# Gather buffers of a sparse graph layer, and the place where a sign matrix is made

## The chip, the cores and the metric

The kernel runs on one core of a Trainium2 chip. The metric is the device time of one execution in microseconds (us); less is better. A core has five engines that each run their own stream of instructions in order: TensorE (PE), VectorE (DVE), ScalarE (ACT), GpSimd (POOL) and SyncE (SP), which wait for each other through semaphores. SP, ACT and POOL also issue DMAs.

## The reference, cut to what matters

Four graph layers, each wrapped as `x = layernorm(x + layer(x, adj))`, on 2708 nodes with 512 features. `adj` is sparse: a random pattern with the diagonal set, weights from 0.05 to 1, float32.

```python
# layer 0
adj_hat = adj + eye;  d = 1 / sqrt(adj_hat.sum(axis=1))
return (d[:, None] * adj_hat * d[None, :] @ x) @ W.T + b
# layer 1
head = (adj > 0);  head = head / max(sqrt(sum(head * head, axis=-1)), 1e-12)
inc = adj + head
return (inc @ x) / sum(inc, axis=-1)
# layer 2 (attention over the neighbours, two gates)
h = x @ W_sa;  scores = (h @ a_sa[0, :512])[:, None] + (h @ a_sa[0, 512:])[None, :]
e = where(adj != 0, exp(-leaky_relu(scores, 0.01)), 0)
x_a = e / (sum(e, axis=1) + 1e-5) @ h;   x_b = adj @ (x @ W_gcnb) + b_gcnb
return sigmoid(attn_a * x_a + attn_b * x_b)   # attn_*: gates from adj @ x and x
# layer 3
bw = sign(weight);  ba = max(sign(x), 0)
return relu(adj @ (ba @ bw.T))
```

The sign matrix of this text is `bw`, 512 x 512, kept as bfloat16; `weight` comes transposed as `w3_t`.

## The kernel before, in words

The 2708 rows are cut into 22 blocks of 128 (the last one, number 21, has 20 rows). Layers handle them in the order `sequence = [0, 1, 21, 2, ..., 20]`. Nothing is multiplied as a dense 2708 x 2708 matrix: for each block of destination rows the kernel gathers only those source rows that the block's columns of `adj` use.

Stage 0 reads `adj`, counts and finds the non-zeros, writes the lists of source rows (`index`), gathers the used rows of the transposed `adj` into `packed` (one tile of 128 sources by 128 destinations for every gathered group), and projects `x` to `y_rows` in DRAM. The order inside this stage is written out (`in_order`); everywhere else each engine's order is made by a list scheduler from the order of the code, the dependencies and the buffers that pools have free. An operation that the code names late can therefore be put early if its buffers and inputs allow it.

Layer 0 and layer 1 have the same core. `gathered` (L626) takes a buffer of the pool's tag `xg` and issues an indirect DMA from POOL, which fetches 128 rows of 512 floats (256 KB) from `y_rows` (layer 0) or `x1_rows` (layer 1; the profile names all of the three `x*_rows` arrays `x_rows`). `add_tile` (L1393) multiplies the tile of `adj` with them into a PSUM tile of the block; a buffer is free again when this product is done. The number of `xg` buffers is the pool's `bufs`: 10 in `s_l0`, 8 in `s_l1`. After every third (layer 0) or second (layer 1) gather, POOL does a short memset (L636) as a pause. Blocks 0 and 1 of the sources are held in SBUF and need no gather.

Beside the products, layer 0's loop runs pieces of other work out of a dictionary `between`, keyed by the step: loads and columns for the attention of layer 2, the counts of positive elements that layer 1 needs (`count_positive`: DVE writes the 0/1 tile `pos` (L1185) and PE counts it, L1187), and `signs(k)` for k = 0 to 3 in steps 8, 10, 12 and 14. `signs` loads a quarter of `w3_t` (256 KB) on ACT's queue into a buffer of the tag `xb` (two of them, pool `work`), and DVE makes the signs in two operations, L1437 (is less than 0) and L1438 (is greater than 0, minus that). `grow1` (L1450 to L1454) adds, a block at a time, to layer 1's sums for block 0, whose sources are all nodes. t (L1508) is layer 0's sum plus the old features; its layer norm follows (L688 to L704).

Layer 1's loop: incidence tiles on DVE (L1674, L1675), products on PE, `finish1` (L1587, the layer norm, the write to `x2_rows`), and for the block before it `project1`: transposes (L1612), the product with `W_sa` (L1619), copies of `h` (L1625 on ACT, L1626 on DVE) and its write (L1627). `grow2` (L1652, L1653) adds to layer 2's sums for block 0.

Layer 2 gathers rows of `x2_rows` with 1028 floats (features, `h` and scores; 514 KB and more for a gather of 128) in `gathered_2` (L1820) into seven buffers and two spare places. `prepare` makes attention weights: ACT adds scores (L1575), DVE does the leaky step (L1576) and the mask (L1578, L1579), ACT the exp (L1580). `accumulate` multiplies both halves of each gathered row (L1844), `transpose2` (L1876) and `project2` (pc L1889, pg and pc L1892) use `W_gcnb` from `s_wg`, 1 MB loaded by ACT's queue at the layer's start (L1724); `finish2` uses the gates, and `sign_product` (L1953) multiplies the signs of the new features with `bw` and writes `xw_rows`. `open_block` makes the row `sl` of left scores (L1553, L1555), and `prepare_own` loads `h_own` on SP's queue. Layer 3 gathers rows of `xw_rows`.

Of the kernel before, what the change touches and what calls it, by code (L numbers as in the profile page):

```python
# [8 lines left out]
F32 = mybir.dt.float32  # L9
F32R = mybir.dt.float32r  # L10
BF16 = mybir.dt.bfloat16
# [3 lines left out]
ALU = mybir.AluOpType  # L15
# [4 lines left out]
P = 128  # L20
# [50 lines left out]
def dense_layers(  # L71
# [30 lines left out]
    NG = -(-N // W)  # L102
    CH = 3
    NFULL = N // P
# [12 lines left out]

    parts = [(j, min(CH, NFULL - j), P) for j in range(0, NFULL, CH)]
    if N % P:
# [53 lines left out]
    def load_until(k: int):  # L173
        while issued[0] <= min(k, 4 * PER_LAYER - 1):
# [3 lines left out]
            w = width(g)  # L178
            t = stream.tile([P, CH, W], F32, tag="adj", name=f"adj{i}")
            nc.sync.dma_start(  # L180
# [327 lines left out]
def sparse_layers(ctx, tc, x, adj, adj_t, w0_t, b0, w_sa, a_sa, w_gcnb, b_gcnb, wa, ba, wb, bb, w3_t,  # L508
# [11 lines left out]
    nc = tc.nc  # L520
    N, D = x.shape
    KC = D // P
    NB = -(-N // P)
# [19 lines left out]
    f = [feat.tile([P, D], F32, tag=f"f{b}", name=f"f{b}") for b in range(NB)]  # L543
# [175 lines left out]
    with tc.tile_pool(name="s_pre", bufs=1) as pre:  # L719
# [65 lines left out]
        turn_at, at = {}, 0  # L785
# [555 lines left out]
    work = ctx.enter_context(tc.tile_pool(name="s_work", bufs=2, side="right", reuse_waits="tile"))  # L1341

    w2 = ctx.enter_context(ExitStack())
    wp = w2.enter_context(tc.tile_pool(name="s_w2", bufs=1, side="right", reuse_waits="tile"))
    bw = wp.tile([P, KC, D], BF16, name="s_bw")
    sequence = [0, 1, NB - 1, *range(2, NB - 1)]


# [56 lines left out]
    with tc.tile_pool(name="s_l0", bufs=10, reuse_waits="tile") as lp:  # L1405
# [24 lines left out]
            for c, side in enumerate((1, 0)):  # L1430
                nc.vector.tensor_copy(wsa[:, :, D + c], vec[:, side, :])

        def signs(k: int):
            w3 = work.tile([P, D], F32, tag="xb", name=f"s_w3_{k}")
            nc.scalar.dma_start(w3, w3_t[k * P : (k + 1) * P, :])
            neg = lp.tile([P, D], F32, tag="scr", name=f"s_neg{k}", bufs=1)
            nc.vector.tensor_scalar(neg, w3, 0.0, None, op0=ALU.is_lt)  # L1437
            nc.vector.scalar_tensor_tensor(  # L1438
                bw[:, k, :], w3, 0.0, neg, op0=ALU.is_gt, op1=ALU.subtract
            )  # L1440

        nc.vector.memset(own1[:, 0:1], 1.0)
        grown1 = []

        def grow1(j: int):
# [14 lines left out]
        between = {  # L1460
            2: [attention_loads], 4: [lambda: attention_columns(0)],
            5: [lambda: attention_columns(1)], 6: [attention_sides],
            8: [lambda: signs(0)], 10: [lambda: signs(1)], 12: [lambda: signs(2)],
            14: [lambda: signs(3)],
        }
        def several(*actions):
            def act():
# [15 lines left out]
        for at, b in enumerate(sequence):  # L1483
# [23 lines left out]
            t = work.tile([P, D], F32, tag="t", name=f"t0_{b}")  # L1507
# [32 lines left out]


    state = {}

    def old_new(b: int):
        return tuple(pairs.get(b, (f[b], f[b])))
# [44 lines left out]
        layernorm(new[:m, :D], t, m, f"1_{b}", on_act=True)  # L1590
        nc.sync.dma_start(x2_rows[b * P : b * P + m, :D], new[:m])

    with tc.tile_pool(name="s_l1", bufs=8, reuse_waits="tile") as lp:
        def gate_columns(dst, c: int, pool, tag: str):

            pv = pool.tile([P, D], F32, tag=tag, name=f"pv2_{c}")
            nc.tensor.transpose(pv[:, : 2 * KC], vrows[:, c, :], ident[: 2 * KC, : 2 * KC])
            nc.vector.tensor_copy(
                dst.rearrange("p k t -> p t k"),
                pv[:, : 2 * KC].rearrange("p (t k) -> p t k", t=2),  # L1600
            )

        gate_columns(wsa[:, :, D + 2 :], 0, ps_mm, "mm")
        H = D // 2
        hs = {}

        def project1(j: int):

            m = rows(j)
            pt = ps_mm.tile([P, KC, P], F32, tag="sum0", name=f"xt1p_{j}", bufs=1)  # L1610
            for k in range(KC):
                nc.tensor.transpose(pt[:, k, :m], f[j][:m, k * P : (k + 1) * P], ident[:m, :m])  # L1612
            xt = lp.tile([P, KC, P], F32, tag="xt1", name=f"xt1_{j}", bufs=2)
            nc.scalar.copy(xt[:, :, :m], pt[:, :, :m])  # L1614
            p0 = ps_acc.tile([P, D], F32, tag="a1", name=f"h0_{j}")
            p1 = ps_acc.tile([P, D], F32, tag="e1", name=f"h1_{j}")
            for ps, w in ((p0[:m, :H], wsa[:, :, :H]), (p1[:m, : H + EXTRA], wsa[:, :, H:])):
                for k in range(KC):
                    nc.tensor.matmul(  # L1619
                        ps, xt[:, k, :m], w[:, k, :], start=(k == 0), stop=(k == KC - 1)  # L1620
                    )
            h = kept[j] if j < 2 else lp.tile(
                [P, D + EXTRA], F32, tag="h", name=f"h_{j}", bufs=4
            )
            nc.scalar.copy(h[:m, :H], p0[:m, :H])  # L1625
            nc.vector.tensor_copy(h[:m, H:], p1[:m, : H + EXTRA])  # L1626
            nc.sync.dma_start(x2_rows[j * P : j * P + m, D:], h[:m, : D + 2])  # L1627
            nc.vector.tensor_copy(cols[:m, j, :], h[:m, D:])
            hs[j] = h

        grown2 = []

        def grow2(js):

            r, n, st = rows(js[0]), len(js), state[0]
            e = lp.tile([P, G2, P], F32, tag="e0", name=f"e0_{js[0]}", bufs=2)[:r, :n, :]
            mask = lp.tile([P, G2, P], F32, tag="mask0", name=f"m0_{js[0]}", bufs=1)[:r, :n, :]
            a = packed[0][:r, js[0] : js[0] + n, :]
            weights_of(
                e, mask, [(e, mask, st["sl"][:r], a, [cols[:r, j, 0:1] for j in js])]  # L1640
            )
            for i in range(n):
                if grown2 or i:
                    nc.vector.tensor_tensor(
                        st["esum"][:r], st["esum"][:r], e[:, i, :], op=ALU.add
                    )
                else:
                    nc.vector.tensor_copy(st["esum"], e[:, i, :])
            for i, j in enumerate(js):
                at = dict(start=(not grown2), stop=(len(grown2) == NB - 1))  # L1650
                se, sa = st["sums"]
                nc.tensor.matmul(se, e[:, i, :], hs.pop(j)[:r, :D], **at)  # L1652
                nc.tensor.matmul(sa, a[:, i, :], f[j][:r], **at)  # L1653
                grown2.append(j)

        G2 = 2
        left = [(0, 1), (NB - 1,)] + [
            tuple(range(j, min(j + G2, NB - 1))) for j in range(2, NB - 1, G2)
        ]

        for at, b in enumerate(sequence):
            m = rows(b)
            if b:
                nd = len(direct(b))
                order_ = in_turns(b)
                src = {i: place_of_x(direct(b)[i]) for i in range(nd)}
                for i in order_:
                    if i >= nd:
                        src[i] = gathered(lp, D, x1_rows, b, i - nd)
                ps = ps_mm.tile([P, D], F32, tag="mm", name=f"l1_{b}")  # L1670
                inc_of = {}

                def incidence(iv, a, row):
                    nc.vector.scalar_tensor_tensor(iv, a, 0.0, row, op0=ALU.is_gt, op1=ALU.mult)  # L1674
                    nc.vector.tensor_tensor(iv, iv, a, op=ALU.add)  # L1675

                for i0, n in whole_runs(b, 3):
                    inc = lp.tile([P, 3, P], F32, tag="inc0", name=f"inc{b}_{i0}", bufs=3)
                    iv = inc[:, :n, :m]
                    incidence(  # L1680
                        iv, packed[b][:, i0 : i0 + n, :],
                        head_row[:, None, b * P : b * P + m].to_broadcast([P, n, m]),
                    )
                    for i in range(n):
                        inc_of[i0 + i] = iv[:, i, :]
                inc = lp.tile([P, P], F32, tag="inc1", name=f"incn{b}", bufs=3)
                for i0, r0, w, a in narrow_views(b):
                    n = a.shape[1]
                    at_ = b * P + r0
                    iv = inc[:, r0 : r0 + n * w].rearrange("p (n i) -> p n i", n=n)  # L1690
                    incidence(
                        iv, a,
                        head_row[:, at_ : at_ + n * w].rearrange("p (n i) -> p n i", n=n),
                    )
                    for i in range(n):
                        inc_of[i0 + i] = iv[:, i, :]
                for i in order_:
                    add_tile(ps, b, i, inc_of[i], src[i][:, :D], order_)
            else:
                ps = sum1  # L1700
            if left and left[0][-1] in sequence[: max(at - 2, 0)]:
                grow2(left.pop(0))
            finish1(b, ps)
            if at:
                project1(sequence[at - 1])
            if at == 1:
                open_block(0, wp2, ps_mm, "mm")
                open_sums(0)
        project1(sequence[-1])
        for js in left:  # L1710
            grow2(js)
# [5 lines left out]
    with tc.tile_pool(name="s_l2o", bufs=1, reuse_waits="tile") as op, \  # L1717
# [5 lines left out]
        wg = op.tile([P, KC, D + 2], F32, name="s_wg")  # L1723
        nc.scalar.dma_start(wg[:, :, :D], w_gcnb.rearrange("(k p) o -> p k o", p=P))  # L1724
        gate_columns(wg[:, :, D:], 1, ps_s2, "sm")
        CH = 3

        def parts_of_sums(b: int):
# [501 lines left out]
```

## Time and profile before

| | before |
|---|---|
| median of three runs | 988.28 us (986.34, 988.28, 994.11) |
| profiled execution | 992.0 us |
| span of its instructions | 990.3 us |
| mean granted TensorE clock | 0.946 |
| PE busy | 860.8 us, 87% of the span, 3659 instructions |
| DVE busy | 654.7 us, 66% |
| POOL busy | 549.4 us, 55% |
| ACT busy | 381.1 us, 38% |
| moved by DMA | 220.06 MB, mean 222 GB/s |
| the chain that ended last | PE 68%, DVE 14%, DMA 7%, issue 5%, ACT 2% |
| gathers of layer 0, of layer 1 | 98 of 997 ns, 98 of 978 ns on POOL |
| L1437 and L1438 | 4 each, 456 ns and 674 ns on DVE |

The stages in the trace: stage 0 to about 200 us, layer 0 to 352, layer 1 to 570, layer 2 to 870, layer 3 to the end.

How to read it: the profile is of one execution, so its durations are summed against 992.0 us, not against the median. "Busy" counts the time in which an engine runs an instruction. A wait has the form "waiting engine, what it was to make, its line <- releasing engine, what that made, its line"; a timeline line has its start, its duration, and in brackets the idle time of the engine before it with what ended that. "issue" is time in which an engine waited for nothing that the profile shows. Tile names are the program's with buffer numbers left out.

### The profile page before, as it was taken

The numbers are of one execution on the slowest core, as the hardware profiler recorded it, in microseconds if no ns is written. First come the engines' busy times: TensorE is split into PE (matmuls) and PEld (weight loads), VectorE is DVE, ScalarE is ACT, GpSimd is POOL, SyncE is SP. The second block draws the span as 40 slices with busy tenths as digits, with TensorE's granted clock in tenths as the row PEclk, the third lists the DMA queues.
The fourth block names the chain that finished last, engine by engine and source line by source line (L and its number), as shares of the span: only waits on it lengthen the run. The fifth ranks groups of instructions, "written<-read, shape, count | busy, mean of one in ns | idle before, by whom it ended". The sixth has DMA issues, their size and how long they took to land.

```text
span 990.3 us, 12880 instructions
## 1 busy us (share of the span) xinstructions
PE 860.8 (87%) x3659; PEld 452.2 (46%) x3659; DVE 654.7 (66%) x2538; ACT 381.1 (38%) x822; POOL 549.4 (55%) x660
## 2 busy tenths in 40 slices
PE   1898789759979979999999989988999999599992
PEld 0444344212222324555555634543555555378771
DVE  4888888726657766565654446675888776556685
ACT  2665556100000014554544433333444333254653
POOL 2577888687877647776542054553454320066661
PEclk9998998979989989999999998998999999889996
DMA  9999996466777646777653276786777541299985
GB/s 266 339 336 306 301 310 199 142 193 192 237 211 222 207 132 195 223 220 233 183 176 121 97 249 236 257 276 216 249 274 261 174 149 47 85 316 331 308 249 173
DMA packets 93557, 220.06 MB, mean 222 GB/s; under 512 B 13660, under 2 KB 28364, under 8 KB 93476
## 3 DMA queue, kind: packets, MB, share of 16 engines
q0 software_dynamic: 43008, 127.61, 43.5%
q1 hardware_dynamic: 38520, 76.78, 22.6%
q10 hardware_dynamic: 11948, 14.76, 4.7%
q8 instruction: 31, 0.51, 0.2%
q14 instruction: 50, 0.41, 0.1%
HBM read 178.21 MB, written 31.71 MB: 212 GB/s over the span
## 4 chain that ended last, share of the span: by engine, by line
PE 68%; DVE 14%; DMA 7%; issue 5%; ACT 2%; another core or an unknown queue 2%; POOL 1%; SPq 0%; ACTq 0%; DVEq 0%; POOLq 0%
PE l L1393 17%; PE h L1619 8%; PE e L1844 7%; PE a L1844 7%; PE l L2099 4%; PE pg L1892 4%; PE pc L1892 3%; PE y L1127 3%; PE l L2138 2%; PE l L1454 2%; PE e L1652 2%; PE a L1653 2%; PE px L1953 2%; DVE s_mask L895 2%; DMA xg<-x_rows,i 2%
## 5 line engine op out<-in xcount | busy, mean ns | idle before, releaser
L1093 POOL DMA_INDIRECT a<-in_adj_t_dram,row_at x98 | 111.3, 1136 | 58.7 <-DVE deg L838 26.1
L626 POOL DMA_INDIRECT xg<-x_rows,i x98 | 95.8, 978 | 70.7 <-PE l L1393 37.1
L626 POOL DMA_INDIRECT xg<-y_rows,i x98 | 97.7, 997 | 32.6 <-issue 19.0
L1393 PE MATMUL l<-xg,a 128*32 128x512 f32 (+3 forms) x196 | 86.0, 646 | 12.6 <-DMA xg<-y_rows,i 12.6
L1820 POOL DMA_INDIRECT xg<-x_rows,i x60 | 59.1, 986 | 61.8 <-ACT ae L1575 16.3
L1127 PE MATMUL y<-s_w,xt 128*128 128x512 f32 (+1 forms) x176 | 91.3, 667 | 1.7 <-ACT xt L1119 1.7
L626 POOL DMA_INDIRECT xg<-xw_rows,i x70 | 71.3, 1018 | 38.7 <-issue 15.9
L1820 POOL DMA_INDIRECT a<-x_rows,i x38 | 36.9, 970 | 95.1 <-DVE mask L1578 37.1
L1619 PE MATMUL h<-s_wsa,xt 128*128 128x256 f32 (+3 forms) x352 | 81.9, 385 | 0.0
L1619 PEld LDWEIGHTS h<-s_wsa,xt 128*128 128x128 f32 (+1 forms) x352 | 63.9, 186 | 24.8 <-ACT xt L1614 9.2
L830 ACT ACTIVATE unused<-arow 128x1408 uint8<-128x1408 f32 (+3 forms) x44 | 58.3, 1325 | 3.0 <-DMA x_rows<-s_zero 2.0
L663 ACT ACTIVATE rsqs<-mv 128x1 f32<-128x1 f32 (+2 forms) x56 | 11.3, 202 | 120.7 <-DVE mv L692 58.8
L1844 PE MATMUL a<-xg,a 128*32 128x512 f32 (+2 forms) x120 | 51.2, 629 | 4.3 <-DMA xg<-x_rows,i 4.3
L1127 PEld LDWEIGHTS y<-s_w,xt 128*128 128x128 f32 (+1 forms) x176 | 35.6, 213 | 41.9 <-issue 39.6
L2099 PE MATMUL l<-ws,pw 128*128 128x512 f32 (+1 forms) x210 | 50.8, 394 | 1.7 <-issue 1.2
L1844 PE MATMUL e<-xg,ae 128*32 128x512 f32 (+2 forms) x120 | 47.9, 601 | 1.1 <-issue 1.1
L694 POOL TENSOR_TENSOR rs<-mv,s_neg_half 128x1 f32<-128x1 f32 (+1 forms) x22 | 13.0, 592 | 61.4 <-DVE mv L692 52.0
L1892 PE MATMUL pg<-s_wg,pt 128*128 128x256 f32 (+1 forms) x176 | 45.0, 397 | 1.3 <-ACT pt L1880 1.3
L688 DVE BATCH_NORM_STATS2 st<-t 128x6 f32<-128x512 f32 (+1 forms) x66 | 45.3, 687 | 0.3
L916 PE MATMUL find<-s_sides,s_mask 128*128 128x5 bf16 (+1 forms) x462 | 15.7, 166 | 34.1 <-DVE s_mask L912 25.2
L2099 PEld LDWEIGHTS l<-ws,pw 128*128 128x128 f32 (+1 forms) x210 | 39.4, 190 | 11.9 <-issue 2.9
L1393 PEld LDWEIGHTS l<-xg,a 128*32 128x32 f32 (+3 forms) x196 | 19.8, 146 | 54.4 <-issue 38.6
(307 smaller groups left out, 1995.5 us busy)
## 6 DMA issues: line engine op xcount, KB each, us to landing
arow<-in_adj_dram SPq DMA_DIRECT2D x21, 704.0 KB
arow<-in_adj_dram SPq DMA_DIRECT2D x21, 650.0 KB
x_rows<-f SPq DMA_DIRECT2D x40, 256.0 KB
aw<-in_adj_t_dram SPq DMA_DIRECT2D x21, 320.0 KB
y_rows<-yt ACTq DMA_DIRECT2D x20, 256.0 KB
x_rows<-h SPq DMA_DIRECT2D x19, 257.0 KB
f<-in_x_dram SPq DMA_DIRECT2D x19, 256.0 KB
h_own<-x_rows SPq DMA_DIRECT2D x19, 256.0 KB
```

The lines of the kernel that those rows point to most:

```text
L626: nc.gpsimd.indirect_dma_start(out=t, out_offset=None, in_=src[:, :], in_offset=bass.IndirectOffsetOnAxis(ap=index[b][:, i : i + 1], axis=0),)
L688: nc.vector.bn_stats(st[:m], t[:m])
L830: nc.scalar.activation(unused[:m, : ar.shape[1]], ar, AF.Copy, accum_out=row_sums[:m, b, h : h + 1])
L895: nc.vector.tensor_scalar(mask[:m, c0 : c0 + ar.shape[1]], ar, 0.0, None, op0=ALU.not_equal)
L1093: nc.gpsimd.indirect_dma_start(out=packed[b][:, t + len(direct(b)), :], out_offset=None, in_=adj_t, in_offset=bass.IndirectOffsetOnAxis(ap ...
L1127: nc.tensor.matmul(ps[:m], xt[:, k, :m], w0[:, k, :], start=(k == 0), stop=(k == KC - 1))
L1393: nc.tensor.matmul(ps[r0:r1], weights, moving, start=(i == order[0]), stop=last_of(b, i, order))
L1619: nc.tensor.matmul(ps, xt[:, k, :m], w[:, k, :], start=(k == 0), stop=(k == KC - 1))
L1820: nc.gpsimd.indirect_dma_start(out=g, out_offset=None, in_=x2_rows[:, :], in_offset=bass.IndirectOffsetOnAxis(ap=index[b][:, t : t + 1], a ...
L1844: nc.tensor.matmul(ps[r0:r1], weights, moving, start=(i == order[0]), stop=last_of(b, i, order))
L1892: nc.tensor.matmul(ps, pt[:, k, :m], w[:, k, :], start=(k == 0), stop=(k == KC - 1))
L2099: nc.tensor.matmul(whole[b], p[:r, h, b * P : (b + 1) * P], g[:r, :], start=(j == 0 and h == 0), stop=(j == NB - 1 and h == 1),)
```

## The change

There are two parts. The pool of layer 1 has twelve buffers instead of eight; only the tag `xg` uses the pool's own number. And `bw` (4 KB of each of the 128 partitions) is no longer in a pool that is open from layer 0 on, but in layer 2's pool `s_l2o`: `signs` runs in layer 2's first steps. The loads of `w3_t` are on SP's queue instead of ACT's; the first two are named in steps 16 and 17 of layer 1's loop, the other two after the first two pairs of sign operations, since the tag `xb` has two buffers. The four gather buffers take 8 KB of each partition.

```diff
     wp = w2.enter_context(tc.tile_pool(name="s_w2", bufs=1, side="right", reuse_waits="tile"))
-    bw = wp.tile([P, KC, D], BF16, name="s_bw")
     sequence = [0, 1, NB - 1, *range(2, NB - 1)]
...
-        def signs(k: int):
-            w3 = work.tile([P, D], F32, tag="xb", name=f"s_w3_{k}")
-            nc.scalar.dma_start(w3, w3_t[k * P : (k + 1) * P, :])
-            neg = lp.tile([P, D], F32, tag="scr", name=f"s_neg{k}", bufs=1)
-            nc.vector.tensor_scalar(neg, w3, 0.0, None, op0=ALU.is_lt)
-            nc.vector.scalar_tensor_tensor(
-                bw[:, k, :], w3, 0.0, neg, op0=ALU.is_gt, op1=ALU.subtract
-            )
...
-            8: [lambda: signs(0)], 10: [lambda: signs(1)], 12: [lambda: signs(2)],
-            14: [lambda: signs(3)],
...
+    w3_of = {}
+
+    def load_w3(k: int):
+        w3_of[k] = work.tile([P, D], F32, tag="xb", name=f"s_w3_{k}")
+        nc.sync.dma_start(w3_of[k], w3_t[k * P : (k + 1) * P, :])
...
-    with tc.tile_pool(name="s_l1", bufs=8, reuse_waits="tile") as lp:
+    with tc.tile_pool(name="s_l1", bufs=12, reuse_waits="tile") as lp:
...
             if at:
                 project1(sequence[at - 1])
+            if at in (NB - 6, NB - 5):
+                load_w3(at - (NB - 6))
...
         gate_columns(wg[:, :, D:], 1, ps_s2, "sm")
+        bw = op.tile([P, KC, D], BF16, name="s_bw")
+
+        def signs(k: int):
+            w3 = w3_of.pop(k)
+            neg = work.tile([P, D], F32, tag="t", name=f"s_neg{k}")
+            nc.vector.tensor_scalar(neg, w3, 0.0, None, op0=ALU.is_lt)
+            nc.vector.scalar_tensor_tensor(
+                bw[:, k, :], w3, 0.0, neg, op0=ALU.is_gt, op1=ALU.subtract
+            )
+
+        for k in range(KC):
+            signs(k)
+            if k + 2 < KC:
+                load_w3(k + 2)
         CH = 3
```

## The prediction

> **What bounds the kernel now.** I read the busy table by stage first, then the waits of layer 1, then the same for layer 0 and for the step from layer 1 to layer 2, because those are the three places that the diff touches. Busy time by stage (the row's first number after the window is its length, then each engine's busy time and number of instructions, the granted TensorE clock, the DMA share and GB/s; the rows are stage 0, layer 0, layer 1, layer 2, layer 3):
>
> ```profile
> 0.00:200.00 200.00, 145.54 (x912) 75.89 (x912) 160.59 (x741) 98.07 (x178) 139.76 (x194) 0.93 0.85 273
> 200.00:352.00 152.00, 129.99 (x399) 38.54 (x399) 92.78 (x417) 9.06 (x37) 112.19 (x130) 0.91 0.70 206
> 352.00:570.00 218.00, 212.06 (x787) 115.14 (x786) 118.17 (x456) 100.61 (x173) 117.97 (x148) 0.98 0.59 178
> 570.00:870.00 300.00, 273.18 (x1150) 144.23 (x1149) 207.67 (x706) 112.69 (x313) 110.32 (x123) 0.95 0.62 206
> 380.00:410.00 30.00, 30.00 (x118) 15.27 (x118) 18.55 (x71) 16.97 (x29) 22.61 (x28) 1.00 0.73 209
> 440.00:470.00 30.00, 30.00 (x124) 16.62 (x123) 16.64 (x66) 14.83 (x27) 21.16 (x27) 1.00 0.76 230
> ```
>
> The reader is to see that layer 1 is a stage of PE: 212 of 218 us busy, and 30.00 of 30.00 in its middle, at full clock. Layer 0 is not: 130 of 152 us. The waits of layer 1 (sum, times, longest) and POOL's timeline at its start:
>
> ```profile
> POOL xg L626 <- PE l L1393: 37.1, 16, 6.8
> ...
> 370.36 0.95 POOL L626 DMA_INDIRECT xg<-x_rows,i  x1 [0.16 <-issue]
> ...
> 386.21 0.94 POOL L626 DMA_INDIRECT xg<-x_rows,i  x1 [3.15 <-PE l L1393]
> ```
>
> So POOL really waits 37.1 us for buffers there, the wait that twelve buffers aim at. But the ninth gather (370.36) passes without a wait, and the first buffer wait comes at 386 us, when PE already has no gap. The waiter is an engine with 118 of 218 us of work, and the engine that it waits for is the full one.
>
> Layer 0's losses, by waits of PE and of POOL in that stage, and the same two-matmul group at two clocks:
>
> ```profile
> PE l L1393 <- DMA xg<-y_rows,i: 12.6, 1, 12.6
> PE l L1454 <- DVE t L1508: 4.4, 1, 4.4
> PE hr L1187 <- DVE pos L1185: 1.9, 2, 1.7
> ...
> POOL xg L626 <- PE l L1393: 8.7, 13, 2.2
> POOL xg L626 <- PE hr L1187: 2.0, 4, 1.2
> POOL xg L626 <- PE hr L1231: 1.9, 2, 1.6
> ...
> 331.47 0.18 PE L1187 MATMUL hr<-s_sides,pos 128*128 128x1 bf16 x1 [1.67 <-DVE pos L1185]
> 334.21 2.08 PE L1393 MATMUL l<-f,a 128*128 128x512 f32 x2
> 337.96 1.02 PE L1393 MATMUL l<-xg,a 128*128 128x512 f32 x2
> ```
>
> POOL issues 98 gathers there (98 at 997 ns, page) from 199.6 to 344.5 us; PE is full from 340 to 352. The stage's length is POOL's stream plus its roughly 13 us of waits (8.7 + 2.0 + 1.9 and small ones) plus PE's tail. And at 328 to 336 us PE waits for DVE's `pos` and then runs at half clock.
>
> **What the Trainium skill says.** "Perfetto Trace Analysis", Identifying Performance Opportunities: a bubble that repeats can mean too few buffers, if it is on the engine that should be saturated. The trace agrees with the condition, against the change: the 37.1 us of bubbles are on POOL. "TensorE: Matmul & The Clock Gate", Part 1: The HAM clock gate: an idle PE falls to half clock and gets it back after some 3.4 us of work; here one form takes 2.08 us after the stall and 1.02 later. "DMA: Bandwidth & Descriptors", Issuing engines are not separate DMA queues: loads issued by SP, ACT and POOL share the same 16 engines and interleave, so moving a load to SP's queue doesn't take it off the others' bandwidth. The 0.83 DMA share at 570 to 580 us, below, fits that, but doesn't isolate it.
>
> **The change part by part.** The sum is made against the profiled execution: 992.0 us, span 990.3; the median, 988.28, is 3.7 lower, and the sum is carried over to it.
>
> *Twelve buffers.* The layer-1 instructions and their order on each engine are unchanged; only the buffer that a gather waits for differs. POOL runs four gathers, about 4 x 1.3 = 5 us, further ahead, and most of the 37.1 us may go. PE lost 2.2 us from 380 to 571, summed over its gaps, and none of these is a wait for a gather. Before 380 it loses some 6 us while the first gathers arrive, and these do not wait for buffers. Cost 0; bounds 0 to -1. What is late next is PE, as before.
>
> *Sign work out of layer 0.* Four times 0.456 + 0.674 us (L1437, L1438) = 4.5 us of DVE, at 248, 260, 275 and 301 us, go, as do two 256 KB loads at 246 and 260 us. DVE has 93 of 152 us; a pair delays a block's chain by at most 1.1 us, and PE was full from 240 to 260. So the 4.5 us themselves are worth about 1. But the scheduler packs the rest otherwise: the DVE order changes from the fifth block on, `pos` (L1185) and the incidence columns (L1450, L1453) come earlier, also ahead of t_14 and t_16. That aims at the stall of 328 to 336: 0.46 + 1.67 idle, and about 2 us of half clock, with POOL's 4.85 us of waits from 331 to 341 behind it. If `pos` is there in time, the gather stream ends 4 to 5 us sooner and PE's tail with it. A bound from above is the 13 us of POOL's waits; from below, +2, that the new order makes a stall of the same kind elsewhere. I take -5: the one stall whose cause the order removes, and a part of a us for the pairs. The stall of 4.4 us at 278 I leave: DVE was idle before t there, so no DVE work is its cause.
>
> *Loads of w3 0 and 1.* They were ACT's tenth and twelfth DMAs at 17 us, and are SP's 33rd and 38th, among stage 0's adjacency loads; the code names steps of layer 1 but the buffer is free from the start. Same 0.5 MB in a stage with 0.85 DMA share: 0 (bounds -0.5 to +0.5).
>
> *Sign work into layer 2's start.* Neg 0 (0.42) stands behind the last block's L1587, ahead of its statistics; the block's features were ready at 554.3 and PE took them at 558.6, so 4 us cover it. Bw 0 and 1 (1.35 us) stand ahead of sl (567.77) on DVE, which had idled 2.09 us just before at 566.4: 0 to +1. Neg 2 and neg 3 each wait for a load of 256 KB that SP issues only when bw 0 and bw 1 have freed the two buffers; behind neg 3 on DVE stands L1576 of the first part (568.8 before), whose scores ACT exponentiates and PE multiplies (585.0). DVE idled 9.49 us behind it, so there is room of some 9 us until PE needs it. SP also holds h_own of the next blocks behind these two loads; they are wanted at the end of a block only.
>
> *The load of w_gcnb.* 1 MB on ACT's queue moves from 562.0 to behind the exp of e_20, about 566. It landed in 563.3 to 566.6 on idle DMA engines; now it and 0.5 MB of w3 run beside h_20's write and the first gathers. The profile there:
>
> ```profile
> 570.00:580.00 10.00, 5.12 (x15) 2.66 (x14) 0.77 (x2) 1.71 (x4) 7.56 (x9) 0.94 0.83 282
> ...
> 569.21 0.95 POOL L1820 DMA_INDIRECT a<-x_rows,i  x1 [36.81 <-DVE mask L1578]
> 571.71 0.94 POOL L1820 DMA_INDIRECT xg<-x_rows,i  x1 [0.30 <-issue]
> ...
> 570.87 1.13 PE L1892 MATMUL pg<-s_wg,pt 128*128 128x256 f32 x4 [0.57 <-ACT pt L1880]
> 571.84 1.88 PE L1844 MATMUL e<-s_h,ae 128*128 128x512 f32 x4
> 578.04 1.40 PE L1844 MATMUL a<-xg,a 128*128 128x512 f32 x2 [4.32 <-DMA xg<-x_rows,i]
> ```
>
> The gather that PE waits for is now the second, not the third (one `a` gather goes behind seven xg): -1.25 us. Against it 0.5 to 1.5 MB more at about 410 KB/us (what flowed at 577 to 585) share the engines: +1 to +3 on its landing. And PE's order puts that gather's product ahead of pg and e<-s_h: about 3 us of work that lay in the wait comes behind it. PE then has work until the loss is paid: the filler is moved, not added, but up to 3 us of it were free. On the other side xg products come ahead of pg and pc, so places for the next gathers are free about 2 us sooner, and POOL waited 6.21 us for these at 586.3. Taken together +1, bounds -2 to +6.
>
> *Layers 2 and 3 after that.* The same work by the same bounds; bw is in place long before the first sign product. 0, bounds -2 to +2.
>
> Sum: 0 - 5 + 0 + 1 + 0 = -4, so 988 for the profiled execution, 984.0 for the median.
>
> **Rivals.** About 1% (9.9 us) is what a measurement of this kernel can tell from no change.
>
> A, nothing moves: layer 1 has no gap to fill, and sign work is hidden in both places. For it: 30.00 of 30.00, DVE's spare 59 us in layer 0. Against: DVE's order does change where PE waited for DVE. 988.
>
> B, layer 0 sheds nearly all its POOL waits: -12 with the seam at 0 gives 976. For it: each stall also costs half clock. Against: the waits of 278 and 217 to 221 us don't hang on sign work.
>
> C, slower: PE enters layer 2 empty-handed. With its 3 us of filler put behind the first gather and that gather later by 1 to 3 for the loads, PE idles about 6.5 us in one piece and then runs some us at half clock (+2 to 3): +3 + 2.5 + 1.5 - 1.25 = +6, and layer 0 gives nothing: 994. It decides if w3's last load lands after about 576, since DVE's first part stands behind it; with layer 0 a further 2 worse it ends beyond 996.
>
> D, the change doesn't do what it says: POOL's waits shrink or move, while PE's times in layer 1 stay equal. I hold that for likely in the forecast itself; as the whole story it gives A's 988.
>
> **How the numbers follow.** Forecast (layer 0 gives 3 to 8, seam within +-2): 0.40, at 984. A with D: 0.20. B: 0.25. C: 0.15. Range: B's 976 less 2, to C's 994 plus 2: 974 to 996, which leaves out the far sides of both. Faster by over 1% (below 978.4): most of B and a tenth of the forecast and of the unknown, 0.30. Slower by over 1% (above 998.2): the far part of C, with a worse order in layer 0, 0.12. Within: 0.58.
>
> **What would show it right or wrong.** Right: POOL's wait for L1393 in layer 1 falls well below 37 us, while PE's gap sum there stays at 2 to 3 us; the end of layer 0 comes 3 to 8 us sooner, with no half-clock stretch behind a wait for `pos`; the first xg product of layer 2 starts 14 us, give or take 2, after DVE's copy of the last block's h (before: 563.71 to 578.04). Wrong: layer 1 gets shorter by more than 1 us (then the gathers did bound PE), layer 0 keeps its length or has a stall as long elsewhere, or layer 2's start shows a DMA wait above 6 us and half clock behind it.

## The result, and the profile after

| | before | changed | ratio, 95% interval |
|---|---|---|---|
| median of 22 runs each | 992.32 us | 988.89 us | 0.999, 0.9972 to 1.0008 |
| profiled execution, span | 992.0, 990.3 us | 986.78, 984.6 us | |

The change of time is within what can be told from none: -1 us by the ratio, with -2.8 to +0.8 as its interval. (The medians lie 3.4 us apart; the runs of one kernel scatter over 13 to 17 us.) -4 was forecast. The sign and the range held, but hardly any of the forecast's terms was right. The lines of the changed kernel that answer to those shown of before follow; in its numbering add_tile is L1392, grow1's product L1444, t of layer 0 L1496, h L1612, layer 2's products L1853 and pg L1901. First waits: POOL's in layer 1, then PE's in layer 0, then PE's behind the start of layer 2 (sum, times, longest):

```profile
POOL xg L626 <- PE l L1392: 34.1, 16, 6.8
```

```profile
PE hr L1187 <- DVE pos L1185: 9.7, 5, 3.9
PE l L1392 <- DVE t L1496: 4.4, 1, 4.4
```

```profile
PE a L1853 <- DMA xg<-x_rows,i: 5.2, 1, 5.2
```

POOL's wait for buffers fell by 3 us only, from 37.1: POOL gets ahead by four gathers once, and then waits as often as before. In layer 0 the waits for `pos`, which were to go, are longer. Next the start of layer 2, POOL's first two gathers and PE's first gathered product in the timeline:

```profile
569.65 0.95 POOL L1829 DMA_INDIRECT a<-x_rows,i  x1 [40.48 <-DMA h_own<-x_rows]
570.91 0.98 POOL L1829 DMA_INDIRECT xg<-x_rows,i  x1 [0.30 <-PE a L1853]
...
577.91 2.08 PE L1853 MATMUL a<-xg,a 128*128 128x512 f32 x2 [5.20 <-DMA xg<-x_rows,i]
```

The reader sees the forecast picture (xg second, pg moved behind it, half clock: 2.08 us where the same form takes 1.02), and yet a shorter way to it: from PE's last product of layer 1 (568.65) to 577.91 it is 9.3 us, where before it was 11.8.

To compare stages I cut each trace at the same events: POOL's first gather of y, PE's last product of grow1, PE's last product of layer 1 (a<-f), PE's first gathered product of layer 2, and the last one. "Start" below is from layer 1's last product to layer 2's first gathered one. Times depend on the chip: the kernel before takes some 990 us on one and 963 on two others, so only kernels of one chip stand side by side. The chip of the first pair isn't on record; by its times I count it with the chip of 990 us.

| us | stage 0 | layer 0 | layer 1 | start | layer 2 |
|---|---|---|---|---|---|
| 990: before | 199.6 | 158.2 | 208.4 | 11.8 | 268.1 |
| 990: changed | 196.2 | 159.7 | 212.8 | 9.3 | 263.1 |
| 990: changed, third profile | 198.9 | 159.2 | 212.9 | 9.4 | 261.8 |
| 963: before, again | 194.2 | 146.3 | 209.0 | 12.0 | 262.7 |
| 963: changed, again | 193.1 | 146.4 | 209.3 | 9.6 | 262.2 |

### The profile page after: what moved, and what is told of

Same layout as the page of the kernel before. It is cut to its first block, busy times and chain, and to the rows that moved or that the text cites. A ratio compares the mean times of both kernels' runs of the same rounds, so it can differ in the third digit from the quotient of the medians.

```text
span 984.6 us, 12880 instructions
## 1 busy us (share of the span) xinstructions
PE 858.4 (87%) x3659; PEld 452.3 (46%) x3659; DVE 657.0 (67%) x2538; ACT 381.3 (39%) x822; POOL 549.2 (56%) x660
## 4 chain that ended last, share of the span: by engine, by line
PE 66%; DVE 15%; DMA 7%; ACT 4%; issue 4%; another core or an unknown queue 4%; POOL 1%; ACTq 0%; DVEq 0%; SPq 0%; POOLq 0%
PE l L1392 14%; PE h L1612 8%; PE e L1853 7%; PE a L1853 6%; PE l L2108 5%; PE l L2147 4%; PE pg L1901 4%; PE pc L1901 3%; DMA arow<-in_adj_dram 3%; PE e L1645 2%; PE l L1444 2%; PE a L1646 2%; PE px L1962 2%; DVE s_mask L895 2%
## 5 line engine op out<-in xcount | busy, mean ns | idle before, releaser
L1392 PE MATMUL l<-xg,a 128*32 128x512 f32 (+3 forms) x196 | 85.3, 642 | 12.7 <-DMA xg<-y_rows,i 10.9
L1612 PE MATMUL h<-s_wsa,xt 128*128 128x256 f32 (+3 forms) x352 | 83.4, 390 | 1.9 <-ACT xt L1607 1.9
L1612 PEld LDWEIGHTS h<-s_wsa,xt 128*128 128x128 f32 (+1 forms) x352 | 64.2, 187 | 28.0 <-ACT xt L1607 12.0
L830 ACT ACTIVATE unused<-arow 128x1408 uint8<-128x1408 f32 (+3 forms) x44 | 58.3, 1325 | 1.5 <-DMA arow<-in_adj_dram 0.6
L1853 PE MATMUL a<-xg,a 128*32 128x512 f32 (+2 forms) x120 | 50.6, 614 | 5.2 <-DMA xg<-x_rows,i 5.2
L1853 PE MATMUL e<-xg,ae 128*32 128x512 f32 (+2 forms) x120 | 48.9, 601 | 1.2 <-issue 1.2
L1392 PEld LDWEIGHTS l<-xg,a 128*32 128x32 f32 (+3 forms) x196 | 20.4, 150 | 56.2 <-issue 40.7
L1901 PE MATMUL pg<-s_wg,pt 128*128 128x256 f32 (+1 forms) x176 | 44.5, 394 | 1.1 <-ACT pt L1889 1.1
L916 PE MATMUL find<-s_sides,s_mask 128*128 128x5 bf16 (+1 forms) x462 | 15.6, 166 | 34.0 <-DVE s_mask L912 25.1
```

The source lines that it names most:

```text
L830: nc.scalar.activation(unused[:m, : ar.shape[1]], ar, AF.Copy, accum_out=row_sums[:m, b, h : h + 1])
L1392: nc.tensor.matmul(ps[r0:r1], weights, moving, start=(i == order[0]), stop=last_of(b, i, order))
L1612: nc.tensor.matmul(ps, xt[:, k, :m], w[:, k, :], start=(k == 0), stop=(k == KC - 1))
L1853: nc.tensor.matmul(ps[r0:r1], weights, moving, start=(i == order[0]), stop=last_of(b, i, order))
L1901: nc.tensor.matmul(ps, pt[:, k, :m], w[:, k, :], start=(k == 0), stop=(k == KC - 1))
```

## Experiments

**Which part does it: eight buffers in the changed kernel, ten in the one before, and both kernels again.** One chip of 963 us. The first two are clean cuts: the order of instructions on every engine is that of the kernel that they come from.

```diff
 signs_only:   changed kernel, -  name="s_l1", bufs=12   +  name="s_l1", bufs=8
 buf10_only:   kernel before,  -  name="s_l1", bufs=8    +  name="s_l1", bufs=10
```

> The changed kernel with eight buffers in layer 1, not twelve; the order of instructions on every engine is that of the changed kernel. My theory (layer 1 is bound by PE, so buffers are worth nothing): the time of the changed kernel, within 0.3%, so 0.996 to 1.001 of the kernel before; POOL's wait for layer 1's products is 35 to 40 us. Rival (the twelve buffers are what gains): 1.000 or above, and the changed kernel is at least 3 us faster than this. Other rival (deeper gathering disturbs PE in layer 1, which is 4 us longer in the profile of the changed kernel): this is some 4 us faster than the changed kernel and layer 1 is back to the length of before.

> The kernel before with ten buffers in layer 1 (twelve don't fit while the sign matrix is kept); order on every engine as before. My theory: 0.997 to 1.003, POOL's 37 us of waits for layer 1's products shrink or are moved, PE's time in layer 1 stays within 2 us. Rival (buffers gain): 0.995 or below, with layer 1 shorter. Rival (deeper gathering disturbs PE): layer 1 longer by some 2 us.

> The changed kernel once more, for a second profile and a comparison on the same chip. If the stage differences of the first pair of profiles are the change's (stage 0 3 us shorter, layer 1 4 us longer, layer 2 5 us shorter), they return here within 1 us. If they are differences between executions, they scatter by as much as they are large. Time 0.997 to 1.001.

> The kernel before once more: 1.000 within 0.2%, and a second profile whose stage lengths tell how far two executions of the same kernel differ: under 1 us in each stage if the first pair of profiles can be read stage by stage, 2 to 5 us if not.

Measured: signs_only 0.9983 (0.9967 to 0.9999), buf10_only 1.0 (0.9986 to 1.0014), after_again 0.9967 (0.9952 to 0.9982), before_again 1.0004 (0.999 to 1.0017). Layer 1 took 208.4, 208.0, 209.3 and 209.0 us. So buffers gain nothing that this can tell, and layer 0 is the same with sign work and without: 146.3 (before_again) and 146.4 (after_again), with 148.7 and 148.4 in the other two, so that two executions differ by 2 us and more there. Two differences come back in all four profiles: PE's first projection at 27.3 and 27.6 us in the kernels before against 24.9 and 25.1, of which 1.1 to 1.8 us are left at layer 0's first gather, and the start of layer 2, 12.0 and 11.5 against 9.6 and 9.5. Neither is a gain that I forecast.

**The two places, each alone.** The timelines of ACT say what to try. Before, then changed, at the start of stage 0:

```profile
17.25 0.35 ACTq L1435 DMA_DIRECT2D s_w<-in_w_t_dram  x1
17.65 1.29 ACT L830 ACTIVATE unused<-arow 128x1300 uint8<-128x1300 f32 x1 [2.00 <-DMA x_rows<-s_zero]
...
21.40 0.34 ACTq L1435 DMA_DIRECT2D s_w<-in_w_t_dram  x1
21.79 0.27 ACT L1011 CAST steps<-find 128x125 bf16<-128x125 f32 x1 [2.76 <-DMA x_rows<-s_masked]
```

```profile
15.55 1.29 ACT L830 ACTIVATE unused<-arow 128x1300 uint8<-128x1300 f32 x1
16.74 0.19 ACT L830 ACTIVATION_READ_ACCUMULATOR unused<-arow 128x1 f32 x1
17.84 0.27 ACT L1011 CAST steps<-find 128x125 bf16<-128x125 f32 x1 [0.91 <-PE find L1002]
```

Each w3 load on ACT's queue stood until a DMA that reads s_zero or s_masked had landed. From that I take it that its buffer lies where those tiles were. ACT is in order, so its counting (L830) and the path to the first projection (L1011) stood behind it, 2.0 and 2.8 us of idle time. SP issues the same two loads at 42.8 and 49.5 us (after_again), when those DMAs have long landed. The second trial holds the 1 MB load of w_gcnb where the changed kernel has it, and leaves sign work in layer 0.

```diff
 w3_sp_in_before:      -  nc.scalar.dma_start(w3, ...)   +  nc.sync.dma_start(w3, ...)
 wg_behind_in_before:     nc.scalar.dma_start(wg[:, :, :D], ...)
                       +  tc.add_manual_dep(<this load>, <exp of e_20 on ACT>, NoSync)
```

> The kernel before with one word changed: the four loads of w3 are issued by SP, not by ACT. The first two then leave ACT's queue, where each stood for 2.1 and 1.4 us waiting for earlier DMAs that read the memory of their buffers. Theory (the changed kernel's first projection comes 2.3 us sooner because ACT no longer stands behind these two loads): first projection at about 25 us, not 27.4, first gather of layer 0 about 1 us sooner, time 0.997 to 1.000. Rival (it is the bytes of the loads, or something else in the change): first projection stays at 27 to 28 us. The rest of the kernel as before, the first gathered product of layer 2 about 11.8 us behind layer 1's last product.

> The kernel before, with the 1 MB load of w_gcnb held behind the last exp of layer 1's block 20 on ACT's queue, where the changed kernel has it; sign work stays in layer 0. Theory (the load stood in the way of the last write of h, and its place alone makes layer 2 start 2.3 us sooner): from layer 1's last product to layer 2's first gathered product 9.5 us, not 11.8; POOL's first gather of layer 2 about 3.5 us behind DVE's last copy of h, not 5.2; time 0.996 to 0.999. Rival (the sign work or the moved w3 loads changed the start): 11.5 to 12 us, time 1.000.

Measured on the chip of 990 us: w3_sp_in_before 0.998 (0.9957 to 1.0003), first projection at 25.2 us, start of layer 2 at 11.5 us as before. wg_behind_in_before 0.9948 (0.9918 to 0.9978), start of layer 2 in 8.3 us, first projection 27.0. Each place makes its own difference in the profile, without sign work moved and without buffers; in time only the second is clear of none. For the second the way is in the DMA queues. The 1.66 us behind SP's issue of the last write of h, in before_again, then in wg_behind_in_before (packets, MB, share; q10 carries ACT's load of w_gcnb, q1 SP's DMAs, the write of h first):

```profile
q10 hardware_dynamic: 327, 0.67, 103.7%
```

```profile
q1 hardware_dynamic: 154, 0.28, 57.9%
```

Where the 1 MB had been issued 2.2 us ahead of it, no byte of h moves in that time, and the last lands 1.6 us later than with the load held back. So from DVE's copy of the last h to POOL's first gather it was 5.2 us in before_again, 3.5 in after_again and 3.7 in wg_behind_in_before. The rest is order: the gather that PE waits for is the second, not the third (1.4 us). In after_again 0.7 us go back, since that gather takes 7.3 us from its issue to PE's product, not 6.6: 1.7 + 1.4 - 0.7 is the 2.4 us by which its start is shorter. The hold isn't a cut as clean as the first two: from layer 1's end on the scheduler makes another order of the first blocks of layer 2 on PE, DVE, ACT and POOL, and the place of that gather is part of it.

**Further along the same way: loads later, the wait filled.** w3_late ties the first two loads to where the code names them. filled also puts pg, pc and the products of the kept h ahead of the first gathered product, and sign work 2 and 3 behind block 1.

```diff
 w3_late:  changed kernel   nc.sync.dma_start(w3_of[k], ...)
                         +  if k < 2: tc.add_manual_dep(<this load>, <write of x2_rows before it>, NoSync)
 filled:   w3_late       +  transpose2(0); project2(0)        # ahead of layer 2's loop
                         +  tc.add_manual_dep(<first gathered product>, <last of project2(0)>, NoSync)
                         +  signs(2); signs(3)                # behind block 1
 filled8:  filled        -  bufs=12                           +  bufs=8
```

> The changed kernel, with the first two loads of w3 tied behind layer 1's writes of blocks 15 and 16 on SP's queue, where the code names them, not in stage 0. They take 0.5 MB out of stage 0, which moves some 270 KB/us. Theory: first gather of layer 0 another 0 to 1.8 us sooner than in the changed kernel, the rest the same, 0.995 to 0.998 of the kernel before. Rival (stage 0 is bound by DVE and ACT at its end, so these bytes are hidden): the time of the changed kernel.

> w3_late, and in layer 2's start the eight products of pg and pc for block 0 and the two of e with the kept h put ahead of the first gathered product, and the sign work of quarters 2 and 3 behind block 1, so that nothing on DVE waits for a load in front of the first attention weights. The 5.5 us in which PE waits for the first gathered rows are then mostly filled: theory: layer 2's first block ends 3 to 5 us sooner, 0.991 to 0.995. Rival (the products wait for the 1 MB of w_gcnb, which the changed kernel loads late, or layer 2 gives it back in a later wait for gathers): same as w3_late within 1 us.

w3_late took 0.9992 (0.9965 to 1.002): 0.5 MB less in stage 0 gains nothing that can be told; its first gather of layer 0 was at 199.0 us. filled took 0.9994 (0.9971 to 1.0018). Of the mechanism half was right: from layer 1's last product to block 1's last gathered products it needed 23.5 us and w3_late 26.5, the 3 us forecast. But the 21st product of a gathered tile of features (a<-xg) stood at 50.5 and 50.7 us, so they were gone again by then, as the rival had it; a wait of PE for sl in filled alone, 2.4 us at 603.8, is a part of that. The whole of layer 2 with its start took 271.8 us in filled, and 272.4 and 271.2 in the changed kernel. And its layer 1 took 215.4 us. All three profiles of twelve buffers on this chip had a long layer 1 by then (212.8, 212.0, 215.4), and the three of eight had 208.4 to 209.0. Hence the next runs, on the same chip:

> The kernel called filled (w3 loads late, pg, pc and e of block 0 ahead of the first gathered product) with eight buffers in layer 1. Its block 1 of layer 2 ended 3 us sooner than in w3_late, but its layer 1 was 6 us longer than with eight buffers. Theory: with eight buffers layer 1 is back at 208 to 210 us and the time is 0.991 to 0.995, faster than the kernel before and the changed one. Rival (the long layer 1 was chance, or a later wait takes the 3 us back): 0.997 to 1.000.

> The changed kernel a third time, against signs_only_2 in the same call. On one chip its layer 1 was 212.8 us with a wait of 1.9 us of PE for ACT, in two other kernels with twelve buffers 212.0 and 215.4, and 208.4 to 209.0 in three kernels with eight; on the other chip 209.3 with twelve and 208.4 to 209.0 with eight. If twelve buffers cost something, layer 1 is 2 us or more longer than in signs_only_2 again on the chip of 990 us; if it was chance, within 1 us. Time 0.996 to 0.999 of the kernel before.

> The changed kernel with eight buffers a second time, for the comparison with after_3. Layer 1 at 208 to 209 us; time within 0.2% of after_3 if buffers are worth nothing, 0.2 to 0.5% below it if twelve disturb PE.

filled8 0.9931 (0.9902 to 0.9961) with layer 1 at 208.3; after_3 0.9969 (0.9947 to 0.9992) with 212.9; signs_only_2 0.9943 (0.9921 to 0.9966) with 209.4. So on this chip twelve buffers lengthen layer 1 by 3 to 7 us in four profiles of four (eight buffers: 208.3 to 209.4 in six), and against signs_only_2 they cost 2.6 us in the ratio, though those two intervals overlap. Where: ACT and PE of the changed kernel (first fence), then of signs_only_2 (second), timelines at the same products:

```profile
380.43 3.75 PE L1612 MATMUL h<-s_wsa,xt 128*128 128x256 f32 x16
384.01 3.60 PE L1392 MATMUL l<-xg,inc 128*128 128x512 f32 x8
386.52 0.37 ACT L1618 COPY s_h<-h 128x256 f32<-128x256 f32 x1 [4.94 <-PE l L1392]
391.94 1.47 PE L1612 MATMUL h<-s_wsa,xt 128*20 128x256 f32 x3 [1.92 <-ACT xt L1607]
```

```profile
380.54 3.73 PE L1612 MATMUL h<-s_wsa,xt 128*128 128x256 f32 x16
382.55 0.37 ACT L1618 COPY s_h<-h 128x256 f32<-128x256 f32 x1 [0.83 <-PE h L1612]
384.10 3.60 PE L1392 MATMUL l<-xg,inc 128*128 128x512 f32 x8
```

The same copy starts 2.0 us behind the first of PE's products of h in one and 6.1 us in the other, although PE's records go on without a gap. What ACT waits for comes late, ACT's next copy with it (in order), and PE idles 1.92 us. It is so in all: from ACT's first copy of h in layer 1 to its second it is 8.2 to 12.2 us in the four profiles of twelve buffers and 7.1 to 7.3 in the six of eight. Why PE's signal is late there isn't settled.

**The two places together.** Kernel before, both edits of w3_sp_in_before and wg_behind_in_before, no other edit; then again on a chip of 963 us with ten and six buffers, and without sign work: both_nosigns loads no w3 and fills the sign matrix with ones in one memset. both_moves has 4 runs, both_moves_2, both_buf10 and both_nosigns 6 each.

> The kernel before with only two DMAs placed otherwise: the loads of w3 issued by SP, and the load of w_gcnb behind the last exp of layer 1. Eight buffers, sign work in layer 0. Theory (these two places are all that the change gains): first projection at 25 us, 8 to 9.6 us from layer 1's last product to layer 2's first gathered one, and the time of the changed kernel within 0.3%, 0.994 to 0.998. Rival (moving the sign work or the buffers carries part of the gain): slower than the changed kernel by 0.3% or more.

> both_moves once more. If its 0.9862 stands: 0.984 to 0.990 on the chip of 990 us; on the chip of 963 us, where PE's signals are never held up, 0.995 to 0.998. If those few runs were favourable ones: 0.992 to 0.997 on either.

> both_moves with ten buffers in layer 1, not eight; every order as in both_moves. If gathering further ahead is what holds PE up on the chip of 990 us: layer 1 at 210 to 213 us there, against 208 to 209.5 in both_moves_2, and the time 0.2 to 0.4% above it. If only twelve, or chance: layer 1 and the time as in both_moves_2. On the chip of 963 us: no difference.

> both_moves with six buffers in layer 1. Theory (PE bounds layer 1, a gather lands about 2.6 us behind its issue and PE uses one every 2 us, so six are ample): layer 1 within 1 us of both_moves_2, POOL's waits for layer 1's products the same or more. Rival (eight were just enough): layer 1 longer by over 2 us, with waits of PE for gathers.

> both_moves without the loads of w3 and the sign work; one DVE memset in layer 0 stands in for the sign matrix, so that the last layer's product is of ones. Theory (sign work in layer 0 is hidden): layer 0 within 2 us of both_moves_2 and the time within 0.2%. Rival (the prediction's step: sign work upsets DVE's order and with it 5 us of layer 0): layer 0 shorter by 3 us or more, 0.3% or more faster.

| | ratio to before | layer 0 | layer 1 | start | layer 2 |
|---|---|---|---|---|---|
| both_moves (990) | 0.9862 (0.9834 to 0.989), 979.46 us | 156.6 | 208.9 | 8.4 | 259.9 |
| both_moves_2 (963) | 0.9908 (0.9879 to 0.9938), 955.63 us | 148.4 | 208.6 | 7.9 | 260.0 |
| both_buf10 (963) | 0.9924 (0.99 to 0.9948) | 148.3 | 208.7 | 8.9 | 256.3 |
| both_buf6 (963) | 1.0011 (0.9998 to 1.0023) | 147.8 | 218.2 | 8.2 | 258.2 |
| both_nosigns (963) | 0.9924 (0.9902 to 0.9946) | 148.1 | 209.2 | 9.0 | 262.4 |

Two DMAs in other places beat both kernels, and by more than the change did: against the changed kernel beside it (after_3, 989.0 us) both_moves is 9.5 us faster. I had expected the two to be equal. Part of it is layer 1, 212.9 us with twelve buffers and 208.9 with eight; against signs_only_2, the changed kernel with eight, it is 7.2 us. On the chip of 963 us the intervals of both_moves_2 and after_again (0.9952 to 0.9982) don't meet either. For the rest the profile offers the start of layer 2, PE's timeline in both_moves:

```profile
568.78 1.10 PE L1900 MATMUL pg<-s_wg,pt 128*128 128x256 f32 x4 [0.91 <-ACT ae L1582]
569.72 1.88 PE L1852 MATMUL e<-s_h,ae 128*128 128x512 f32 x4
572.19 1.12 PE L1852 MATMUL a<-xg,a 128*128 128x512 f32 x2 [0.59 <-DMA xg<-x_rows,i]
574.98 1.12 PE L1852 MATMUL a<-xg,a 128*128 128x512 f32 x2 [1.66 <-DMA xg<-x_rows,i]
```

Without sign work and its loads on DVE in front of the first weights, 3 us of pg and e fill the wait, the rest is 0.59 and 1.66 us, and the gathered pair runs in 1.12 us, not at half clock. From layer 1's last product to the end of block 1's last it is 24.9 us there and 24.8 in both_moves_2, 26.9 in after_again and 28.7 in before_again. At the 21st product a<-xg the lead of both_moves_2 over before_again is 8.1 us (45.1 against 53.2), of which a wait of PE for sl, 2.3 us in before_again and none in both_moves_2, is a part; near layer 2's end 6.8 us are left. That this start is the whole reason isn't shown. both_nosigns has the same order of products there and waits hardly longer, but its second pair runs at half clock:

```profile
557.24 1.13 PE L1861 MATMUL a<-xg,a 128*128 128x512 f32 x2 [1.19 <-DMA xg<-x_rows,i]
560.05 2.08 PE L1861 MATMUL a<-xg,a 128*128 128x512 f32 x2 [1.68 <-DMA xg<-x_rows,i]
```

Its block 1 ends at 27.9 us only, and yet its time is that of both_moves_2 within the intervals. both_nosigns keeps layer 0 (148.1 against 148.4) and the time: sign work in layer 0 costs nothing. Of buffers, ten are as good as eight and six too few, by 9.7 us of layer 1. (Its order differs in a few instructions at layer 1's start.) Its waits of PE for gathers are only 3.4 us, and eight buffers have 1.8 of these too, so they name little of the loss (first fence; the second is busy time in one stretch of layer 1, its own and that of both_moves_2):

```profile
PE l L1393 <- DMA xg<-x_rows,i: 3.4, 4, 1.8
```

```profile
370.00:400.00 30.00, 29.62 (x104) 12.85 (x103) 16.78 (x66) 15.88 (x26) 21.30 (x27) 1.00 0.66 182
369.00:399.00 30.00, 30.00 (x115) 14.29 (x114) 18.69 (x73) 16.92 (x27) 24.14 (x31) 1.00 0.72 205
```

Both windows begin some 27.8 us into layer 1. PE is 29.62 of 30 us busy with six buffers, and yet has 104 matmuls, where both_moves_2 has 115. So here a PE that is full by the busy share wasn't at its rate. The weight loads tell it too (second engine of the row): 12.85 us against 14.29. How the missing buffers slow PE without a gap in its records isn't shown.

## Why the prediction was right or wrong

- **Twelve buffers, 0 (0 to -1).** No gain: right, and shown by buf10_only and by signs_only with after_again. Two things were wrong with its working. I bounded it from one side only, and on one chip it costs about 4 us of layer 1. And "30.00 of 30.00 busy" did not prove that buffers gain nothing: six buffers show nearly the same share in one stretch and lose 9.7 us. As far as it rested on that share it was right by luck. Its other ground, that no wait of PE from 380 to 571 us is one for a gather, is better: from 365 us on six buffers have three such waits, and eight have none.
- **Sign work out of layer 0, -5.** This is the step that failed: 0 was measured, by both_nosigns and by before_again with after_again (0.2 us). On the chip of 990 us too, layer 0 took 156.6 to 163.8 us in the four profiles with sign work in it and 156.5 to 159.9 in the six without. The 4.5 us of DVE are hidden, as counted, but the stall at 328 to 331 us that I took as the order's doing was none of DVE's. The trace of before had it:

```profile
328.69 1.10 PE L1393 MATMUL l<-xg,a 128*128 128x512 f32 x2
330.98 0.43 DVE L1185 TENSOR_SCALAR pos<-a 128x512 bf16<-128x512 f32 x1 [1.86 <-PE l L1393]
```

PE's last product before it ended at 329.79, the next event of PE's semaphore lies at 330.96, and `pos` started 0.02 us behind that. Of DVE's 1.86 us of idle time 1.2 are for a late signal of PE's, and an earlier place for `pos` doesn't bring that signal. On the chips of 963 us the same kernel waits 0.8 us for `pos` in this layer.

- **w3 loads from ACT to SP, 0 (-0.5 to +0.5).** Failed: -1.1 to -1.8 at layer 0's first gather on the chip of 963 us, though in the whole time w3_sp_in_before (0.998) can't be told from none. I priced the bytes. They are the same, as the Trainium skill says of DMAs from different engines ("DMA: Bandwidth & Descriptors", Issuing engines are not separate DMA queues: all run on the same 16 engines), and the trace agrees, with a DMA share of 0.85 before and 0.84 after in the first 200 us. What I put at nothing was the wait of the issuing instruction and what stood behind it on ACT.
- **The start of layer 2, +1 (-2 to +6).** Failed in sign for the start itself: -1.9 to -2.5. Its parts: xg second, -1.25 forecast, -1.4 read. The gather's landing, +1 to +3 forecast, +0.7 read. pg behind it, a loss, right in kind: by block 1's end the changed kernel is 0.2 us behind on the chip of 990 us (27.3 to 27.5) and only 1.8 ahead on the other. But the w_gcnb load was taken as traffic added beside h's write, where it was traffic taken out from ahead of it, -1.7. That had no term: I had read the load as landing on idle DMA engines, and h's write stood behind it. Of two transfers that meet I had looked at the later place only.
- **Sum.** -4 forecast. Measured: -1 (-2.8 to +0.8) at first, -3.1 (-5.3 to -0.8) by after_3 on the chip of 990 us, and -3.2 (-4.6 to -1.7) by after_again on that of 963. Where the size is right it is so by luck: on the chip of 963 us 0, 0, about -1.4 and -2.2 where 0, -5, 0 and +1 stood. On the chip of 990 us twelve buffers take part of it back: -5.7 by signs_only_2, with eight. Two slips of its sums change nothing: 988.28 less 4 is 984.3, not 984.0, and its chances leave no share for the "unknown" of which a tenth is counted.
- **Rivals.** A came nearest in the number. C's place and mechanism were there, 5.2 us of idle PE in one piece with half clock behind it, and the sum still was a gain since all came sooner. D was right: the waits shrank by 3 us and PE's time in layer 1 didn't fall.

## What to carry to other kernels

When a load is moved to another queue, look at what stood behind its issue on the old one and what its bytes were in front of, before counting bytes. When a stall is to be removed by a new order, first see that the releaser's own end and the released start lie together; where a microsecond lay between them here, a new order of the waiter's work did not help. A part of a change that gains can be tried by itself: here two DMA placements, with the order that the scheduler made of them, are worth more than the whole.

## What the runs showed that I had not expected

On the chip of 990 us PE's completion signals come late, in the kernel before too. In the semaphore events of its layer 0 they lie at 277.18, 278.62, 280.09 and 281.51 us, while PE's last product there ended at 278.36; DVE's t, which waited for the last of them, started at 281.53, and PE stood 4.43 us. In each of the ten profiles of that chip, in every stage, there are such gaps, 90 to 109 in all, in which a product ended over 0.5 us before the next signal; in the eight of the chips of 963 us there are at most 2. Layer 0 takes 156.5 to 163.8 us on the one chip and 146.3 to 148.7 on the others, which fits, but that the signals are the reason isn't shown.

A caution: on that chip only 645 to 674 of some 800 signals have an event of their own, on the others nearly all, so a gap can be a lost event; sure are those where an engine that waited started late. Such gaps lie early in layer 1 with eight buffers too. With twelve the second copy of h was late each time, with eight never; whether the gathers in flight cause it stays open, since both_buf10 ran on the other chip and twelve buffers don't fit beside the kept sign matrix.
